# Layer 1 of a four-layer graph network: first operands in five pieces, a part's sums issued in front of the dense layers, and stepwise digits in the preparation

## The chip, the cores and the metric

The kernel runs on one core of one Trainium2 chip. The metric is the device time of one execution in microseconds (us), of which lower is better. Three timed executions of the kernel before took 5485.16, 5464.78 and 5445.3 us, so the median is 5464.78. The profile is of a further execution, with a time of its own that is given below.

A core has a tensor engine (PE, with its weight loads shown apart as PEld), a vector engine (DVE), a scalar engine (ACT), GpSimd (POOL) and a sync engine (SP), which here only issues transfers. Each works through its own queue of instructions in order and waits for the others by semaphores.

## The reference

Four graph layers run one after the other on node features x (3125 x 128, f32) and one list of 100000 edges, sorted by destination. Each is added to its input and normalised:

```python
edge_index = jnp.stack([src, dst])
x = layernorm(x + L0(x, z, edge_index, edge_type_500, Wc, P, y, residual_weight))
x = layernorm(x + L1(x, edge_index, W1, b1, W2, b2))
x = layernorm(x + L2(x, edge_index, edge_attr_3, Wq, Wk, Wv, We, Wo, bo, Wm, bm))
x = layernorm(x + L3(x, edge_index, edge_type_8, node_type_4, W_Q, W_K, W_V, W_edge, mu))
```

L0 is attention with 8 heads and an embedding for each of 500 relations: every edge has a logit from its destination's, its source's and its relation's vectors, a softmax runs over a node's incoming edges and the node itself, and the messages are summed. L2 is attention with 4 heads and a bias from three edge attributes, L3 attention with a matrix for each node type and edge type. L1, which the change is mostly about, is a mean over the edges the other way round and a small network:

```python
row, col = edge_index[0], edge_index[1]          # row = src, col = dst
summed = segment_sum(x[col], row)
deg = segment_sum(ones, row)
agg = summed / maximum(deg, 1)[:, None]
return relu(agg @ W1.T + b1) @ W2.T + b2
```

## The kernel before, in words

All is one function, `tile_gnn`, written for a framework that orders the instructions. The function's text gives each instruction a priority in the order in which it is written. A block under `tc.high_priority(offset=AHEAD)`, with AHEAD = 600, is treated as if it stood 600 places earlier, as far as its inputs allow. Tiles come from pools; a tile name with `bufs=2` has two buffers, and a third use waits until the first is released. These rules, and the semaphores that follow from them, set the order on each engine.

**Preparation** (to about 200 us). Edges are sorted into a table `edge_table` by destination; `h_tab` and `z_tab` are tables of node and relation vectors, transformed for layer 0. Nodes are ordered by in-degree into NT = 25 tiles of 128. Tile t has CAP[t] edge slots to a node, from 57 down to 21, in columns OFF[t] to OFF[t+1]; NS = 821 in all. GpSimd gathers the edges of each tile (the payload, `pay_sb`, L504), SP stores all of it to `pay_tab` (L505), and VectorE derives from each tile's payload (L507 to L516) the source `srcx`, a mask, the relation `rel` and the source in a second form, `srcs`. Then, over all 821 columns at once, come L517 to L523: two additions, and the splitting of `srcs` into its low seven bits plus one (`srclo`) and the rest (`srchi`). L525 to L533 turn `rel` into floats (`relf`), transpose it in seven blocks of up to 128 columns on TensorE, convert each on ScalarE and store it to `rel_tab` by SP; two buffers `r16` take turns.

**Counting.** Layer 1 needs a matrix of how many edges lead from each source to each destination. `counts` (L574 to L658) makes it for one tile of destinations by one-hots (L582, L619), a scan (L586), scalings on ScalarE (L623) and matmuls, and stores it to `c_tab`. It is a generator: its steps are issued one by one between the gathers of layer 0.

**behind** (L660 to L686) is a loop over edges that don't fit in a node's slots. The number of trips is read from memory by all engines (`values_load`), so all of them meet there, at L666 and L667. With the given inputs it is zero. For layer 0 it is called at L927, in front of the counting and the tiles.

**Layer 0** (L757 to L1038, to about 2060 us). For each of 25 tiles, GpSimd gathers the rows of sources from `h_tab`, one instruction to a slot (all gathers are recorded at L102); part of the relation vectors come by gathers too, part by one-hot matmuls from `rb`, which SP loads from `rel_tab`. After softmax and layernorm a tile's result goes to `x1_tab`, and its product with W1, split into three bf16 pieces, to `u_tab` (L1038).

**Layer 1** (L1042 to L1163, to about 2239 us). `u1` is all of `u_tab` (L1044, one transfer). A branch (L1057) leads to a general path for graphs for which the counts don't fit; it isn't taken here. Then come the weights: `w2` and its transpose, the bias rows `b1` and `b2`, and `wqkv2` for layer 2. The out-degree becomes `deg1` (L1123), is transposed (`dT`) and stored as one row, `degrow` (L1131); `xn` is the layer's input (L1133). The 3200 columns of sources are worked through in seven parts, CW = 512 columns each and 128 in the last. For each part the counts `cs` are loaded (L1137, two buffers), and 1 + 75 matmuls add up in `y_ps` (two buffers): `b1` times `degrow` (L1140), then 25 tiles x 3 pieces (L1143). VectorE and ScalarE make `hT` of it (L1145, L1146). Each 128 columns then go through the dense layers: a matmul with `w2T` (`o_ps`, L1150), the residual and a layernorm into `xq` (two buffers), a transpose, a matmul with `wqkv2` (`p_ps`), and two stores to `kv_tab` and `xq_tab` (L1162, L1163).

**Layers 2 and 3** gather from these tables and are not touched. Layer 2 opens with gathers of `xqb` from `xq_tab`.

Of the kernel before, what the change touches and what calls it, by code (L numbers as in the profile page):

```python
# [8 lines left out]
F32 = mybir.dt.float32  # L9
F16 = mybir.dt.float16  # L10
BF16 = mybir.dt.bfloat16
I32 = mybir.dt.int32
AF = mybir.ActivationFunctionType
OP = mybir.AluOpType
# [4 lines left out]
P = 128  # L19
N = 3125  # L20
NT = 25
NP = NT * P
# [9 lines left out]
PADREL = 511  # L32
# [10 lines left out]
OFF = [sum(CAP[:t]) for t in range(NT + 1)]  # L43
NS = OFF[NT]
# [7 lines left out]
CW = 512  # L52
NCW = -(-NP // CW)
AHEAD = 600
# [33 lines left out]
def tile_gnn(ctx, tc, a, out):  # L88
    nc = tc.nc
    V, A, G, T = nc.vector, nc.scalar, nc.gpsimd, nc.tensor  # L90
# [22 lines left out]
    ident = const.tile([P, P], F32, name="ident")  # L113
# [378 lines left out]
    rel = slots.tile([P, NS], I32, name="rel")  # L492
    srcx = late.tile([P, NS], I32, name="srcx")
    srclo = slots.tile([P, NS], F32, name="srclo")
    srchi = slots.tile([P, NS], BF16, name="srchi")
    pay_tab = dram.tile([P, NS * PW], I32, name="pay_tab")
    rel_tab = dram.tile([-(-NS // P) * P, P], F16, name="rel_tab")
    with tc.tile_pool(name="srcp", bufs=1) as sp, tc.tile_pool(name="srcq", bufs=2, space=PSUM) as ps:

        pay_sb = sp.tile([P, NS, PW], I32, name="pay_sb")  # L500
        start_i = sp.tile([P, NT], I32, name="start_i")
        V.tensor_copy(start_i, od.start)
        for t in range(NT):
            gather(pay_sb[:, OFF[t]:OFF[t + 1], :].rearrange("p s w -> p (s w)"), edge_tab, start_i[:, t:t + 1])  # L504
        nc.sync.dma_start(pay_tab, pay_sb.rearrange("p s w -> p (s w)"))  # L505
        srcs = sp.tile([P, NS], I32, name="srcs")
        for t in range(NT):  # L507
            sl = slice(OFF[t], OFF[t + 1])
            V.tensor_copy(srcx[:, sl], pay_sb[:, sl, 0])
            live = sp.tile([P, max(CAP)], F32, name="live", bufs=2)  # L510
            V.tensor_scalar(live[:, :CAP[t]], slotid[:, :CAP[t]], od.deg[:, t:t + 1], None, op0=OP.is_lt)
            V.tensor_scalar(mask[:, sl], live[:, :CAP[t]], -NEG, NEG, op0=OP.mult, op1=OP.add)
            V.scalar_tensor_tensor(rel[:, sl], pay_sb[:, sl, 1], float(-PADREL), live[:, :CAP[t]],
                                   op0=OP.add, op1=OP.mult)
            V.scalar_tensor_tensor(srcs[:, sl], pay_sb[:, sl, 0], float(-NP), live[:, :CAP[t]],
                                   op0=OP.add, op1=OP.mult)  # L516
        V.tensor_scalar(rel, rel, float(PADREL), None, op0=OP.add)  # L517
        V.tensor_scalar(srcs, srcs, float(NP), None, op0=OP.add)
        digit = sp.tile([P, NS], I32, name="digit")
        V.tensor_scalar(digit, srcs, 127, None, op0=OP.bitwise_and)  # L520
        V.tensor_scalar(srclo, digit, 1.0, None, op0=OP.add)
        V.tensor_scalar(digit, srcs, 7, None, op0=OP.arith_shift_right)
        V.tensor_copy(srchi, digit)  # L523

        relf = sp.tile([P, NS], F32, name="relf")  # L525
        V.tensor_copy(relf, rel)
        for o in range(0, NS, P):
            n = min(P, NS - o)
            rps = ps.tile([P, P], F32, name="rps")
            T.transpose(rps[:n], relf[:, o:o + n], ident)  # L530
            r16 = sp.tile([P, P], F16, name="r16", bufs=2)
            A.activation(r16[:n], rps[:n], AF.Copy)
            nc.sync.dma_start(rel_tab[o:o + n], r16[:n])  # L533


    c_tab = dram.tile([NCW * P, NT * CW], BF16, name="c_tab")
# [235 lines left out]
    u_tab = dram.tile([P, NT * 3 * D], BF16, name="u_tab")  # L772
# [3 lines left out]
    with tc.tile_pool(name="l0", bufs=2) as wp, tc.tile_pool(name="l0s", bufs=1) as sp, \  # L776
# [147 lines left out]
            spread(ac, hs, lg[:, :W], W)  # L924
            nc.sync.dma_start(sums_at[t], az)

        behind(wp, behind0)  # L927

        up = count_up(cp, ps1)

# [6 lines left out]
        done = 0.0  # L937
        x1st = own(0)
        ahead = x1st, prologue(0, x1st)
        for t in range(NT):  # L940
            n = CAP[t]
# [7 lines left out]
            for run in runs(t):  # L949
                hss = []  # L950
                for s0, w, mult in run:
                    o = OFF[t] + s0
                    if s0 + w == n and t + 1 < NT:

                        ahead = x_next, prologue(t + 1, x_next)
# [85 lines left out]

    with ExitStack() as ctx1, tc.tile_pool(name="l1", bufs=2) as wp, tc.tile_pool(name="l1s", bufs=1) as sp:  # L1042
        u1 = sp.tile([P, NT, 3, D], BF16, name="u1")
        nc.sync.dma_start(u1, u_tab.rearrange("p (t k d) -> p t k d", t=NT, k=3))  # L1044

        more = sp.tile([P, 1], F32, name="more")
        V.tensor_reduce(more, crowd, AX.X, OP.max)
# [9 lines left out]
        with tc.If(general > 0):  # L1057

            with tc.tile_pool(name="l1g", bufs=1) as gp, tc.tile_pool(name="l1gp", bufs=1, space=PSUM) as ps:
# [13 lines left out]
                for t in range(NT):  # L1073
# [27 lines left out]
                    for c in range(NCW):  # L1101
                        w = min(CW, NP - c * CW)
# [5 lines left out]
                for c in range(NCW):  # L1108
                    w = min(CW, NP - c * CW)
# [21 lines left out]
        nc.sync.dma_start(degrow, dT)  # L1131
        xn = sp.tile([P, NT, D], F32, name="xn")
        nc.sync.dma_start(xn, x1_tab.rearrange("(t p) d -> p t d", p=P))  # L1133
        for c in range(NCW):
            w = min(CW, NP - c * CW)
            cs = wp.tile([P, NT, CW], BF16, name="cs")
            nc.sync.dma_start(cs[:, :, :w], c_tab[c * P:(c + 1) * P].rearrange("p (t w) -> p t w", w=CW)[:, :, :w])  # L1137
            y_ps = ps1.tile([P, CW], F32, name="y_ps", bufs=2)

            T.matmul(y_ps[:, :w], b1, degrow[:, c * CW:c * CW + w], start=True, stop=False)  # L1140
            for t in range(NT):
                for k in range(3):
                    T.matmul(y_ps[:, :w], u1[:, t, k, :], cs[:, t, :w], start=False, stop=(t == NT - 1 and k == 2))  # L1143
            hT = wp.tile([P, CW], F32, name="hT")
            V.tensor_add(hT[:, :w], y_ps[:, :w], sums[:, c * CW:c * CW + w])  # L1145
            A.activation(hT[:, :w], hT[:, :w], AF.Relu)  # L1146
# [28 lines left out]
    with tc.tile_pool(name="l2", bufs=2) as wp, tc.tile_pool(name="l2s", bufs=1) as sp, \  # L1175
# [105 lines left out]
        for t in range(NT):  # L1281
            qp = query(ps1, qb[:, t, :])
            for s0, s1, run in segments(t):
                lg = wp.tile([P, max(CAP), H2], F32, name="lg")
                parts = []
                for c0, w in run:
                    o = OFF[t] + c0
# [126 lines left out]
```

## Time and profile before

| what | value |
|---|---|
| timed executions, median | 5464.78 us (5445.3 to 5485.16) |
| profiled execution, its own time | 4502.25 us |
| its span | 4500.4 us |
| instructions | 40304 |
| busy: PE, PEld | 2014.7 us (45%), 1312.7 us (29%) |
| busy: DVE, ACT, POOL | 3035.2 us (67%), 973.0 us (22%), 2845.9 us (63%) |
| mean granted clock of TensorE | 0.699 of full speed |
| transfers | 498.40 MB, mean 111 GB/s |

The stages, as starts of the work of each show them in the timeline (us from the span's start):

| stage | from | to |
|---|---|---|
| preparation | 0 | 200.4 |
| layer 0, with the counting beside it | 200.4 | 2060 |
| layer 1 | 2060 | 2239 |
| layer 2 | 2239 | 3404 |
| layer 3 | 3404 | 4500 |

How to read the profile's lines that follow. In a timeline a line has the start in us, the duration (from the first to the last of a bundle when it ends in "x2" or more), the engine, the line of the source, the operation, what it writes and reads, and, in brackets, how long the engine had waited and for whom. An engine's name with a q, as SPq or ACTq, is its own queue or sequencer: issues of transfers, register reads and branches. In a table of windows each engine has its busy time in the stretch and its number of instructions. Releasers are inferred from semaphores. The profiled execution is over 900 us shorter than the timed ones, and the profile does not say where that lies.

### The profile page before, as it was taken

The numbers are of one execution on the slowest core, as the hardware profiler recorded it, in microseconds if no ns is written. First come the engines' busy times: TensorE is split into PE (matmuls) and PEld (weight loads), VectorE is DVE, ScalarE is ACT, GpSimd is POOL, SyncE is SP. The second block draws the span as 40 slices with busy tenths as digits, with TensorE's granted clock in tenths as the row PEclk, the third lists the DMA queues.
The fourth block names the chain that finished last, engine by engine and source line by source line (L and its number), as shares of the span: only waits on it lengthen the run. The fifth ranks groups of instructions, "written<-read, shape, count | busy, mean of one in ns | idle before, by whom it ended". The sixth has DMA issues, their size and how long they took to land. (4 is left out here: it accounts for less than half of the span.)

```text
span 4500.4 us, 40304 instructions
## 1 busy us (share of the span) xinstructions
PE 2014.7 (45%) x12091; PEld 1312.7 (29%) x12091; DVE 3035.2 (67%) x7206; ACT 973.0 (22%) x2553; POOL 2845.9 (63%) x2897
## 2 busy tenths in 40 slices
PE   6458678877797787896802223233331000000000
PEld 5245455655565465563300011111110000000000
DVE  8649679887788697883336776777762556566566
ACT  0124334433344343331101111111110000000000
POOL 0376546666677365560077777777755777777775
PEclk9678789888898798897955556566665555555555
DMA  2444333434344233354433443344432333333332
GB/s 70 134 115 118 98 88 104 122 108 114 102 132 123 70 113 99 90 129 169 147 97 113 121 129 121 121 129 129 129 105 90 104 104 104 104 103 103 104 102 75
DMA packets 213054, 498.40 MB, mean 111 GB/s; under 512 B 62329, under 2 KB 109100, under 8 KB 208185
## 3 DMA queue, kind: packets, MB, share of 16 engines
q0 software_dynamic: 136448, 397.65, 30.9%
q1 hardware_dynamic: 76344, 97.76, 6.8%
q8 instruction: 102, 1.67, 0.2%
q14 instruction: 160, 1.31, 0.1%
HBM read 424.65 MB, written 70.63 MB: 110 GB/s over the span
## 5 line engine op out<-in xcount | busy, mean ns | idle before, releaser
L102 POOL DMA_INDIRECT hs<-h_tab,srcx x821 | 898.5, 1094 | 552.3 <-issue 346.4
L102 POOL DMA_INDIRECT kv<-kv_tab,pay_sb x821 | 781.3, 952 | 257.8 <-issue 249.3
L102 POOL DMA_INDIRECT kv<-ktv_tab,pay_sb x821 | 777.4, 947 | 263.9 <-issue 258.4
L1351 DVE TENSOR_TENSOR qk<-kv,qp 128x1024 f32<-128x1024 f32 (+4 forms) x114 | 126.8, 1112 | 465.8 <-DMA kv<-ktv_tab,pay_sb 391.8
L728 DVE TENSOR_REDUCE u<-msg 128x128 f32<-128x1024 f32 (+4 forms) x228 | 382.7, 1678 | 0.0
L879 PE MATMUL zps<-oh,zq 128*128 128x512 bf16 x1232 | 365.2, 411 | 34.6 <-DVE oh L870 34.1
L1193 DVE TENSOR_TENSOR qk<-kv,qp 128x1024 f32<-128x1024 f32 (+4 forms) x114 | 126.8, 1113 | 341.4 <-DMA kv<-kv_tab,pay_sb 324.1
L891 PE MATMUL t_ps<-zw,zT 128*128 128x136 f32 x1232 | 210.6, 299 | 113.5 <-DVE hs L892 94.6
L102 POOL DMA_INDIRECT zs<-z_tab,rel x205 | 216.1, 1054 | 64.3 <-issue 56.5
L623 ACT ACTIVATE c_oha<-c_oha,srclo 128x50 bf16<-128x50 bf16 (+2 forms) x821 | 202.3, 327 | 221.0 <-DVE c_oha L619 216.8
L724 DVE TENSOR_TENSOR msg<-kv,ex 128x1024 f32<-128x1024 f32 (+4 forms) x228 | 248.2, 1101 | 0.0
L830 PE MATMUL lg<-yw,low 128*128 128x8 f32 x1642 | 219.1, 260 | 26.2 <-ACT low L828 16.8
L830 PEld LDWEIGHTS lg<-yw,low 128*128 128x128 f32 x1642 | 210.5, 199 | 67.7 <-ACT low L828 51.1
L739 PE MATMUL tp<-ident,an 128*128 128x128 f32 x25 | 11.5, 459 | 486.2 <-DVE an L1239 486.2
L891 PEld LDWEIGHTS t_ps<-zw,zT 128*128 128x128 f32 x1232 | 183.2, 202 | 146.0 <-DVE hs L892 106.3
L883 PE MATMUL pre<-zT,zw 128*128 128x512 f32 x308 | 188.6, 697 | 35.2 <-ACT zT L881 34.6
L885 PEld LDWEIGHTS pre<-ident,hs 128*128 128x128 f32 x1232 | 175.8, 208 | 66.6 <-issue 65.5
L828 ACT ACTIVATE low<-pre 128x512 f32<-128x512 f32 (+2 forms) x215 | 123.0, 573 | 299.5 <-PE pre L885 233.0
L885 PE MATMUL pre<-ident,hs 128*128 128x128 f32 x1232 | 181.1, 292 | 0.0
L821 PE MATMUL pre<-identb,hq 128*128 128x512 bf16 (+3 forms) x645 | 180.3, 372 | 1.3 <-ACT hq L813 0.7
L1263 PE MATMUL xk_ps<-of,xqb 128*128 128x512 f32 x50 | 50.9, 1121 | 278.9 <-DVE xqb L757 270.6
L879 PEld LDWEIGHTS <-zq 128*128 128x128 bf16 x1232 | 128.8, 112 | 121.2 <-issue 61.3
(395 smaller groups left out, 5172.4 us busy)
## 6 DMA issues: line engine op xcount, KB each, us to landing
rb<-rel_tab SPq DMA_DIRECT2D x77, 256.0 KB, 3.3
c_tab<-c_sb SPq DMA_DIRECT2D x25, 768.0 KB, 3.7
cs<-c_tab SPq DMA_DIRECT2D x6, 3200.0 KB, 11.2
hs<-h_tab,srcx POOLq DMA_INDIRECT x821
kv<-kv_tab,pay_sb POOLq DMA_INDIRECT x821
kv<-ktv_tab,pay_sb POOLq DMA_INDIRECT x821
h_tab<-h SPq DMA_DIRECT2D x25, 132.0 KB, 2.3
zs<-z_tab,rel POOLq DMA_INDIRECT x205
```

The lines of the kernel that those rows point to most:

```text
L102: return G.indirect_dma_start(out=dst, out_offset=None, in_=table, in_offset=indirect(idx), **kw)
L623: A.activation(oha[:, s, 0, :], oha[:, s, 1, :], AF.Copy, scale=srclo[:, o:o + 1])
L724: V.tensor_tensor(msg[:, :n, :].rearrange("p s (h d) -> p s h d", h=heads), val.rearrange("p s (h d) -> p s h d", h=heads), ex.unsqueeze(3 ...
L728: V.tensor_reduce(u, msg[:, :n, :].rearrange("p s d -> p d s"), AX.X, OP.add)
L821: T.matmul(pre[:, :k], hq[:, i, :], identb.unsqueeze(1).to_broadcast([P, k, P]), start=(i == 0), stop=False)
L830: T.matmul(lg_ps[:, s, :], low[:, s, :], yw8, start=True, stop=True)
L879: T.matmul(zps, zq[:, i, 2 * R * k2:2 * R * (k2 + 1)], ohs[i][:, cols], start=(i + k2 == 0), stop=(i == NK - 1 and k2 == 1))
L883: T.matmul(pre[:, :k], zw[:, :D], zT[:, cols], start=False, stop=False)
L885: T.matmul(pre[:, s, :], hs[:, s0 + s, :D], ident, start=False, stop=(s == k - 1))
L891: T.matmul(t_ps[:, s, :], zT[:, (s0 + s) * P:(s0 + s + 1) * P], zw[:, D:], start=True, stop=True)
L1193: V.tensor_mul(qk[:, :n], kv[:, :n, :D], qp.unsqueeze(1).to_broadcast([P, n, D]))
L1351: V.tensor_mul(qk[:, :n], kv[:, :n, :D], qp.unsqueeze(1).to_broadcast([P, n, D]))
```

## The change

Three places are edited.

**Preparation.** The work of L517 to L533 becomes a function `digits_of(o, e)`, which does it for columns o to e: relations with their transposes and stores first, then the digits. It is called inside the loop over tiles, whenever another 256 columns are complete, and for the rest after the last tile: 0 to 256, 256 to 512, 512 to 768, 768 to 821.

**The call of `behind`** for layer 0 is put under `tc.high_priority(offset=AHEAD)`.

**Layer 1.** `u1` and the counts of the first part (`cs0`) are loaded in five pieces of five tiles each, in turns, ahead of the branch to the general path. The loading of `cs` and the sums of a part become a function `part(c)`, which returns `y_ps`; the sums of part c + 1 are issued ahead of the dense layers of part c.

```diff
--- before.py
+++ after.py
@@ -504,6 +504,27 @@
             gather(pay_sb[:, OFF[t]:OFF[t + 1], :].rearrange("p s w -> p (s w)"), edge_tab, start_i[:, t:t + 1])
         nc.sync.dma_start(pay_tab, pay_sb.rearrange("p s w -> p (s w)"))
         srcs = sp.tile([P, NS], I32, name="srcs")
+        digit = sp.tile([P, NS], I32, name="digit")
+        relf = sp.tile([P, NS], F32, name="relf")
+
+        def digits_of(o, e):
+
+            V.tensor_scalar(rel[:, o:e], rel[:, o:e], float(PADREL), None, op0=OP.add)
+            V.tensor_copy(relf[:, o:e], rel[:, o:e])
+            for q in range(o, e, P):
+                n = min(P, e - q)
+                rps = ps.tile([P, P], F32, name="rps")
+                T.transpose(rps[:n], relf[:, q:q + n], ident)
+                r16 = sp.tile([P, P], F16, name="r16", bufs=2)
+                A.activation(r16[:n], rps[:n], AF.Copy)
+                nc.sync.dma_start(rel_tab[q:q + n], r16[:n])
+            V.tensor_scalar(srcs[:, o:e], srcs[:, o:e], float(NP), None, op0=OP.add)
+            V.tensor_scalar(digit[:, o:e], srcs[:, o:e], 127, None, op0=OP.bitwise_and)
+            V.tensor_scalar(srclo[:, o:e], digit[:, o:e], 1.0, None, op0=OP.add)
+            V.tensor_scalar(digit[:, o:e], srcs[:, o:e], 7, None, op0=OP.arith_shift_right)
+            V.tensor_copy(srchi[:, o:e], digit[:, o:e])
+
+        done = 0
         for t in range(NT):
             sl = slice(OFF[t], OFF[t + 1])
             V.tensor_copy(srcx[:, sl], pay_sb[:, sl, 0])
@@ -514,23 +535,11 @@
                                    op0=OP.add, op1=OP.mult)
             V.scalar_tensor_tensor(srcs[:, sl], pay_sb[:, sl, 0], float(-NP), live[:, :CAP[t]],
                                    op0=OP.add, op1=OP.mult)
-        V.tensor_scalar(rel, rel, float(PADREL), None, op0=OP.add)
-        V.tensor_scalar(srcs, srcs, float(NP), None, op0=OP.add)
-        digit = sp.tile([P, NS], I32, name="digit")
-        V.tensor_scalar(digit, srcs, 127, None, op0=OP.bitwise_and)
-        V.tensor_scalar(srclo, digit, 1.0, None, op0=OP.add)
-        V.tensor_scalar(digit, srcs, 7, None, op0=OP.arith_shift_right)
-        V.tensor_copy(srchi, digit)
-
-        relf = sp.tile([P, NS], F32, name="relf")
-        V.tensor_copy(relf, rel)
-        for o in range(0, NS, P):
-            n = min(P, NS - o)
-            rps = ps.tile([P, P], F32, name="rps")
-            T.transpose(rps[:n], relf[:, o:o + n], ident)
-            r16 = sp.tile([P, P], F16, name="r16", bufs=2)
-            A.activation(r16[:n], rps[:n], AF.Copy)
-            nc.sync.dma_start(rel_tab[o:o + n], r16[:n])
+
+            whole = OFF[t + 1] if t == NT - 1 else OFF[t + 1] // (2 * P) * 2 * P
+            if whole > done:
+                digits_of(done, whole)
+                done = whole
 
 
     c_tab = dram.tile([NCW * P, NT * CW], BF16, name="c_tab")
@@ -924,7 +933,8 @@
             spread(ac, hs, lg[:, :W], W)
             nc.sync.dma_start(sums_at[t], az)
 
-        behind(wp, behind0)
+        with tc.high_priority(offset=AHEAD):
+            behind(wp, behind0)
 
         up = count_up(cp, ps1)
 
@@ -1041,7 +1051,11 @@
 
     with ExitStack() as ctx1, tc.tile_pool(name="l1", bufs=2) as wp, tc.tile_pool(name="l1s", bufs=1) as sp:
         u1 = sp.tile([P, NT, 3, D], BF16, name="u1")
-        nc.sync.dma_start(u1, u_tab.rearrange("p (t k d) -> p t k d", t=NT, k=3))
+        cs0 = wp.tile([P, NT, CW], BF16, name="cs")
+        for t0 in range(0, NT, 5):
+
+            nc.sync.dma_start(u1[:, t0:t0 + 5], u_tab.rearrange("p (t k d) -> p t k d", t=NT, k=3)[:, t0:t0 + 5])
+            nc.sync.dma_start(cs0[:, t0:t0 + 5], c_tab[:P].rearrange("p (t w) -> p t w", w=CW)[:, t0:t0 + 5])
 
         more = sp.tile([P, 1], F32, name="more")
         V.tensor_reduce(more, crowd, AX.X, OP.max)
@@ -1131,16 +1145,28 @@
         nc.sync.dma_start(degrow, dT)
         xn = sp.tile([P, NT, D], F32, name="xn")
         nc.sync.dma_start(xn, x1_tab.rearrange("(t p) d -> p t d", p=P))
-        for c in range(NCW):
+
+        def part(c):
+
             w = min(CW, NP - c * CW)
-            cs = wp.tile([P, NT, CW], BF16, name="cs")
-            nc.sync.dma_start(cs[:, :, :w], c_tab[c * P:(c + 1) * P].rearrange("p (t w) -> p t w", w=CW)[:, :, :w])
+            cs = cs0 if c == 0 else wp.tile([P, NT, CW], BF16, name="cs")
+            if c:
+                nc.sync.dma_start(cs[:, :, :w], c_tab[c * P:(c + 1) * P].rearrange("p (t w) -> p t w", w=CW)[:, :, :w])
             y_ps = ps1.tile([P, CW], F32, name="y_ps", bufs=2)
 
             T.matmul(y_ps[:, :w], b1, degrow[:, c * CW:c * CW + w], start=True, stop=False)
             for t in range(NT):
                 for k in range(3):
                     T.matmul(y_ps[:, :w], u1[:, t, k, :], cs[:, t, :w], start=False, stop=(t == NT - 1 and k == 2))
+            return y_ps
+
+        ahead = part(0)
+        for c in range(NCW):
+            w = min(CW, NP - c * CW)
+            y_ps = ahead
+            if c + 1 < NCW:
+
+                ahead = part(c + 1)
             hT = wp.tile([P, CW], F32, name="hT")
             V.tensor_add(hT[:, :w], y_ps[:, :w], sums[:, c * CW:c * CW + w])
             A.activation(hT[:, :w], hT[:, :w], AF.Relu)
```

## The prediction

> **What bounds the kernel now.** I read the page first, then the busy time of the engines by stage, the timeline at the two places that the change touches, and the waits. The page's chain of work that ended last goes back only to about 3500 us, into layer 3; it reaches neither edited place, so their worth has to be read from the timeline there.
>
> Busy time by stage (columns: the stretch in us, its length, then for each engine busy us and instructions, then TensorE's granted clock, DMA share, GB/s):
>
> ```profile
> 145.00:178.00 33.00, 1.36 (x4) 0.41 (x4) 20.20 (x149) 0.28 (x1) 23.80 (x25) 0.50 0.51 151
> 178.00:200.40 22.40, 2.66 (x9) 1.35 (x9) 20.80 (x36) 3.11 (x12) 0.00 (x0) 0.50 0.36 136
> ...
> 2060.00:2239.00 179.00, 147.17 (x666) 67.96 (x666) 49.39 (x216) 24.00 (x83) 2.77 (x1) 0.89 0.49 177
> 2239.00:3404.00 1165.00, 305.26 (x578) 137.17 (x578) 758.18 (x1693) 169.97 (x373) 829.71 (x871) 0.58 0.39 120
> ```
>
> From 178 to 200.4 us VectorE works alone (20.80 of 22.40) while GpSimd, which must gather all of layer 0's rows, does nothing. Layer 1, 2060 to 2239, is TensorE's (147.17 of 179). Layers 2 and 3 are left as they were. The timeline of the first place:
>
> ```profile
> 178.25 0.18 DVE L509 COPY srcx<-pay_sb 128x21 int32<-128x21 int32 x1 [1.20 <-DMA pay_sb<-edge_table,start_i]
> ...
> 182.55 0.92 DVE L582 TENSOR_TENSOR c_oh<-srchi,each_j 128x1425 bf16<-128x1425 bf16 x1
> ...
> 194.60 2.35 DVE L586 TENSOR_TENSOR_SCAN c_inc<-c_oh 128x1050 f32<-128x1050 bf16 x1
> ...
> 198.83 1.35 ACT L623 ACTIVATE c_oha<-c_oha,srclo 128x75 bf16<-128x75 bf16 x5 [7.96 <-DVE c_oha L619]
> ...
> 200.46 0.35 POOL L798 MEMSET x<- 128x128 f32 x2 [24.32 <-ACTq L667]
> ```
>
> The engines meet at the loop of `behind` (L667); ScalarE comes last, with counting work, at 200.2, and GpSimd starts layer 0 after 24.32 us of waiting. The second place:
>
> ```profile
> 2060.54 0.32 SPq L1044 DMA_DIRECT2D u<-u_tab  x1
> ...
> 2073.16 3.42 SPq L1131 DMA_DIRECT2D degrow<-dT  x1
> 2076.62 30.89 SPq L1137 DMA_DIRECT2D cs<-c_tab  x3
> 2081.20 5.14 DVE L1151 TENSOR_TENSOR xn<-xn,b 128x128 f32<-128x128 f32 x25 [8.07 <-DMA xn<-x_tab]
> 2081.56 0.50 PEld L1140 LDWEIGHTS y_ps<-degrow,b 1*128 1x128 f32 x2 [9.04 <-DMA degrow<-dT]
> ...
> 2088.95 19.73 PE L1143 MATMUL y_ps<-cs,u 128*128 128x512 bf16 x82 [3.61 <-DMA cs<-c_tab]
> ```
>
> A part's first matmul is L1140, with `degrow`; the first sum (L1143) waits last for `cs`, issued only at 2076.62. Two transfers thus open layer 1, 7 us apart. At its end:
>
> ```profile
> 2218.76 0.69 DVE L1145 TENSOR_TENSOR hT<-y_ps,sums 128x512 f32<-128x512 f32 x1 [10.28 <-PE y_ps L1143]
> ...
> 2234.99 0.32 SPq L1163 DMA_DIRECT2D xq_tab<-xq  x1
> ...
> 2239.01 0.99 POOL L102 DMA_INDIRECT xqb<-xq_tab,node_d  x1 [175.35 <-issue]
> ```
>
> **What the Trainium skill says.** "DMA: Bandwidth & Descriptors", section "Queues, rings and completion order": an engine's descriptors are taken in ring order on each DMA engine, so a small load queued behind a big one comes after it. The trace agrees: the 64 KB bias load issued behind `u1` (2400 KB) took 8.7 us to land, a 128 KB store later 1.7. "Runtime: NRT & Kernel Launch", section "Instruction fetch mechanics": a taken branch to a page not held stalls for its fetch by DMA. The trace agrees: TensorE's jump over the general path (L1057), with `u1` under way, took 6.47 us, those at L329 and L1326 3.50 and 4.63. "TensorE: Matmul & The Clock Gate", Part 1: idle TensorE falls to half clock. The trace agrees: 0.50 in 2060 to 2089, 1.00 from 2107 to 2219.
>
> **The change part by part.** Its instruction order on each engine can be read without running it.
>
> Steps of preparation (L517 to L533). Before, seven full-width operations of 0.58 to 0.59 us, begun 0.50 to 0.61 apart, stand between the last payload (178.25) and the counts' first one-hot (182.55): 4.3 us. After, three of four steps (256 columns) run in VectorE's gaps between payloads. A 256-wide operation I put at 0.28 us (0.18 at 21 columns, 0.58 at 821, a straight line). The third step is held up: its order puts it behind the copy of payload 23, which lands at 176.57; 0.6 us of small operations and seven wide ones, of which two follow the last payload, give a one-hot at about 179.6. Gain 2.9 us.
>
> `behind` in front. VectorE no longer does before the meeting: the 1050-wide scan 2.35, three copies and a subtraction 0.57, three one-hots 0.69 + 0.78 + 0.68: 5.1 us; nor ScalarE its five scalings (1.35). VectorE leaves at 199.65 - 2.9 - 5.1 + 0.9 (the last step's 53-column operations, now between others) = 192.6. The queue of SP: `pay_tab` (2463 KB, 8.0 us) is still issued at 178.5; four of the seven `rel_tab` stores now go ahead of it, the fifth and sixth land behind it at about 187, the seventh waits for a buffer until then and lands at 189.5; `rb`, 3.3 us, lands at 192.9. So the meeting is at 193 to 193.5, not 200.2, and GpSimd starts **6.7 us** earlier. The 5.1 us go behind the meeting, where VectorE stood idle 4.43 us (for `rb`) and 3.88 (for the first rows) and was busy only 36.84 us of 200 to 300, against GpSimd's 76.74. That hides them; without that cover they cost 5.1. From the second tile on the order of layer 0 is the same on every engine, so I carry the shift through: -6.7.
>
> Five pieces. `u1` and part 0's `cs`, 5.73 MB in ten DMAs, go ahead of everything. `u1` flowed at about 0.42 MB/us from 2062.5; so they end at 2076.2. SP's ten issues and two waits for landed pieces bring it to its own jump at 2067 (2063.4 before), past it at 2070 to 2073. Then come `w2`, the biases and `wqkv` behind the pieces: `w2` lands at 2077.5 (about 2071.5 before). TensorE transposes it, then `deg1`; `dT` is ready at 2079.3, `degrow` is issued at 2079.6 and, behind the `xn` load (5.7 us of transfer after 2078.3), lands at 2085.5 instead of 2081.5. L1140 takes 1.9 us at half clock, and the sums begin at 2087.4: **-1.5** against 2088.95. What was late is no longer `cs` but `degrow`. Bounds: -8 (`degrow` does not suffer: 2081), +3 (SP's jump waits for all pieces). Later `cs` parts are issued with a buffer's release and take 11.2 us, under a part's 16: no stall.
>
> Sums in front. The work is the same; only the filling moves. Before, a part ends every 22.4 us with four dense tiles between its sums; without them it takes 75 x 0.213 + 1.1 = 17.1. One part now runs bare: part 5 ends 5.3 us earlier, 6.8 with the start, at 2211.9. But nine dense tiles then remain with only part 6's 4.8 us of short matmuls to cover them, not five. Before, pairs of tiles were stored at 2224.93/2226.32, 2230.04/2231.49 and the single one at 2234.99: 5.0 us a pair (two `xq` buffers), 16.3 us from part 5's end. After: the first pair 4.8 us after the end, the single one 4 pairs later: 4.8 + 20 = 24.8. Layer 1 thus changes by -6.8 + 24.8 - 16.3 = **+1.7**; with TensorE idling towards half clock I take 2.5.
>
> Sum: -6.7 + 2.5 = **-4.2 us**. The profiled execution took 4502.25 us (span 4500.4 and 1.85 around it): 4498. The three timed runs have a median of 5464.78, 962 more, with 40 us between them; the profile does not show where those 962 lie, so I carry the microseconds over: **5461**.
>
> **The rivals.**
> Larger gain: `degrow` slips in early and the dense tiles overlap as pairs of pairs. Then -8 at the start, 4 off the tail: about -16, 5449. Against it: ring order, which delayed `w2` before.
> Slower: layer 1's tail. A tile at half clock costs more (the last `p_ps` took 1.65 us instead of 0.91, a transpose and an output matmul twice theirs: +1.4 a tile). Pairs then take up to 7.8 us, the tail 36, layer 1 +13, the whole **+6**: 5471. It decides from a pair of 6.1 us on. For it: while interleaved, pairs took about 8 us. Against it: at the end before, 5.0.
> Clock: part sums at half clock throughout would cost 450 x 0.213 = 96 us, 5560. Against it: layer 1 ran at 1.00 from 2107 to 2219.
> Change without effect in preparation: the meeting waits for SP's stores behind `pay_tab` as long as before; then only +2.5. This lies inside the forecast's range.
>
> **How the numbers follow.** Forecast (-10 to +3) 0.55; larger gain 0.15; slower tail 0.20; lower clock 0.04; a gain over 1% by a shift in layer 0 that I don't see 0.06. A measurement of this kernel can tell about 1% (55 us) from no change. Hence faster 0.06, within 1% 0.90, slower 0.04. With both tail cases (-16, +6) and some 15 to 20 us of scatter in a median of such runs, the range is 5430 to 5488.
>
> **What would show it.** Right: GpSimd's first memset of layer 0 near 193.5 after a wait of 17 us; the last `rel_tab` store near 187; in layer 1 the first sum waiting for `degrow`, not `cs`; nine dense tiles after the last full part. Wrong: first sum before 2080 (after the shift) or after 2092; layer 0 not 6 to 7 us earlier at its end; a half clock in the part sums.

## The result: no difference that the measurement can tell

The changed kernel takes 5472.66 us (median of 20 runs, 5445.61 to 5494.59), the kernel before 5458.85 (20 runs, 5424.51 to 5485.16). The ratio is 1.0016 with a 95% interval of 0.9999 to 1.0033, so the change costs between nothing and 18 us. In a second comparison (g11 below) it is 1.0005 (0.9986 to 1.0024). The forecast of 5461 and its range hold the time; the first interval leaves no room for the forecast gain of 4.2 us (0.9992), the second does not exclude it.

One thing must be known to read the traces: the same kernel runs at one of two levels, a "short" one (first trace: 4500.4 us) and a "long" one (second trace: 5463.9 us), whatever the change. Layer 1, 178.5 us in the first trace, is 177.8 in the second; layer 0 is 1860 and 2497. So every ratio and every absolute time below is compared within one level.

Busy time by stage of the kernel before in its second trace, e1 below (columns as in the prediction):

```profile
178.00:203.70 25.70, 2.52 (x9) 1.19 (x9) 23.25 (x57) 3.11 (x12) 0.03 (x1) 0.50 0.31 119
2700.00:2878.50 178.50, 147.12 (x666) 67.95 (x666) 49.41 (x216) 24.04 (x83) 2.77 (x1) 0.89 0.49 178
2878.50:4228.00 1349.50, 313.09 (x578) 139.02 (x578) 785.09 (x1698) 170.32 (x374) 830.38 (x871) 0.57 0.33 104
```

The same of the changed kernel:

```profile
178.00:198.10 20.10, 1.30 (x5) 0.59 (x5) 17.99 (x70) 0.76 (x3) 0.01 (x1) 0.50 0.38 147
2692.00:2876.00 184.00, 145.90 (x666) 68.75 (x666) 49.05 (x215) 24.05 (x83) 2.76 (x1) 0.89 0.49 172
2876.00:4221.00 1345.00, 308.22 (x578) 137.19 (x578) 785.73 (x1698) 170.75 (x374) 828.22 (x871) 0.57 0.34 104
```

VectorE does 5.3 us less between 178 us and layer 0's start (17.99 against 23.25), and this stretch is 5.6 us shorter. Layer 1 is some 6 us longer (184.0 against 177.8, first issue to first gather) with the same work in it. In these two stages the change thus gives about as much as it takes. The timeline of the changed kernel at the first place:

```profile
183.85 0.16 DVE L530 COPY srcx<-pay_sb 128x21 int32<-128x21 int32 x1
184.85 0.90 DVE L591 TENSOR_TENSOR c_oh<-srchi,each_j 128x1425 bf16<-128x1425 bf16 x1
...
198.09 0.34 POOL L807 MEMSET x<- 128x128 f32 x2 [21.06 <-DVEq L676]
...
201.92 2.35 DVE L595 TENSOR_TENSOR_SCAN c_inc<-c_oh 128x1050 f32<-128x1050 bf16 x1 [4.54 <-DMA az<-sums_tab]
```

The second scan (2.35 us) has moved behind GpSimd's first memset, which waited 21.06 us instead of 27.0 in the kernel before at this level. The start of layer 1, SP's issues and TensorE:

```profile
2692.27 0.32 SPq L1057 DMA_DIRECT2D u<-u_tab  x1
...
2697.61 0.58 SPq L1058 DMA_DIRECT2D cs<-c_tab  x1
2706.18 0.34 SPq L343 DMA_DIRECT2D w<-in_L_gnn_W  x1
...
2713.55 3.37 SPq L1145 DMA_DIRECT2D degrow<-dT  x1
2721.84 2.07 PE L1157 MATMUL y_ps<-degrow,b 1*128 1x512 f32 x2 [8.63 <-DMA degrow<-dT]
2723.84 18.98 PE L1160 MATMUL y_ps<-cs,u 128*128 128x512 bf16 x75
```

`degrow` is what TensorE waits for, 8.63 us; the sums then follow without a wait for the counts. And the end of layer 1:

```profile
2849.78 0.69 DVE L1171 TENSOR_TENSOR hT<-y_ps,sums 128x512 f32<-128x512 f32 x1 [10.29 <-PE y_ps L1160]
...
2872.25 0.32 SPq L1189 DMA_DIRECT2D xq_tab<-xq  x1
...
2876.28 0.99 POOL L102 DMA_INDIRECT xqb<-xq_tab,node_d  x1 [180.89 <-issue]
```

22.5 us lie between the last full part's result and the last store of `xq`, where the kernel before had 16.2.

### The profile page after: what moved, and what is told of

The parts are those of the page before. It is cut to its first block, busy times and chain, and to the rows that moved or that the text cites. A ratio compares the mean times of both kernels' runs of the same rounds, so it can differ in the third digit from the quotient of the medians.

```text
span 5449.7 us, 40327 instructions
## 1 busy us (share of the span) xinstructions
PE 2158.4 (40%) x12091; PEld 1396.4 (26%) x12091; DVE 3093.7 (57%) x7227; ACT 975.8 (18%) x2553; POOL 2810.8 (52%) x2897
## 5 line engine op out<-in xcount | busy, mean ns | idle before, releaser
L102 POOL DMA_INDIRECT hs<-h_tab,srcx x821 | 842.9, 1027 | 824.6 <-issue 482.5
L102 POOL DMA_INDIRECT kv<-ktv_tab,pay_sb x821 | 801.8, 977 | 322.6 <-issue 262.1
L888 PE MATMUL zps<-oh,zq 128*128 128x512 bf16 x1232 | 392.6, 436 | 68.0 <-DVE oh L879 49.4
L839 PE MATMUL lg<-yw,low 128*128 128x8 f32 x1642 | 237.5, 271 | 94.3 <-issue 48.4
L901 DVE TENSOR_TENSOR hs<-hs,t_ps 128x408 f32<-128x408 f32 (+1 forms) x231 | 121.6, 526 | 266.1 <-PE t_ps L900 98.0
L839 PEld LDWEIGHTS lg<-yw,low 128*128 128x128 f32 x1642 | 230.4, 215 | 139.4 <-ACT low L837 68.2
L656 PE MATMUL c_ps<-c_ohs,c_ohd 128*128 128x128 bf16 x1300 | 138.9, 260 | 257.6 <-ACT c_sb L658 116.2
L579 DVE TENSOR_TENSOR c_ohs<-c_ends,c_up 128x1024 bf16<-128x1024 bf16 (+3 forms) x196 | 115.6, 591 | 203.8 <-remote 153.7
L830 PE MATMUL pre<-identb,hq 128*128 128x512 bf16 (+3 forms) x645 | 201.8, 409 | 10.0 <-ACT low L837 9.4
L656 PEld LDWEIGHTS <-c_ohd 128*128 128x128 bf16 x1300 | 114.4, 118 | 317.9 <-issue 221.6
```

Of the source, the lines that this page charges most:

```text
L102: return G.indirect_dma_start(out=dst, out_offset=None, in_=table, in_offset=indirect(idx), **kw)
L656: T.matmul(cps[:, j * P:(j + 1) * P], ohd[:, b // 2, :, b % 2], ohs[:, b // 2, :, b % 2], start=(i == 0), stop=(i == nb - 1))
L830: T.matmul(pre[:, :k], hq[:, i, :], identb.unsqueeze(1).to_broadcast([P, k, P]), start=(i == 0), stop=False)
L839: T.matmul(lg_ps[:, s, :], low[:, s, :], yw8, start=True, stop=True)
L888: T.matmul(zps, zq[:, i, 2 * R * k2:2 * R * (k2 + 1)], ohs[i][:, cols], start=(i + k2 == 0), stop=(i == NK - 1 and k2 == 1))
```

## The experiments

Four numbers are read from each trace: GpSimd's first memset of layer 0 ("memset"), and for layer 1, counted from the first issue of `u`, the first sum ("start"), from there to the sixth part's `hT` ("middle"), and on to layer 2's first gather ("tail"). In f7 and g9 SP issues the small loads ahead of `u`; these 2.5 us are not counted in "layer 1".

| kernel | level | memset | start | middle | tail | layer 1 | ratio to the kernel before (95%) |
|---|---|---|---|---|---|---|---|
| before, first trace | short | 200.46 | 28.4 | 129.8 | 20.3 | 178.5 | |
| before again (e1) | long | 203.67 | 27.8 | 129.8 | 20.3 | 177.8 | 0.9993 (0.9978 to 1.0007) |
| changed | long | 198.09 | 31.6 | 125.9 | 26.5 | 184.0 | 1.0016 (0.9999 to 1.0033) |
| changed again (g11) | long | 199.28 | 30.5 | 124.7 | 27.4 | 182.6 | 1.0005 (0.9986 to 1.0024) |
| layer 1's part alone (e2) | long | 203.58 | 30.8 | 124.8 | 27.4 | 183.0 | 1.0009 (0.9993 to 1.0026) |
| preparation's part alone (e3) | long | 196.78 | 27.6 | 129.3 | 19.6 | 176.5 | 0.9998 (0.9981 to 1.0015) |
| `behind` alone (e4) | long | 203.66 | 27.1 | 129.7 | 19.4 | 176.2 | 0.9992 (0.9977 to 1.0006) |
| pieces alone (f5) | short | 200.58 | 32.0 | 130.7 | 19.2 | 181.9 | 1.0009 (1.0002 to 1.0016) |
| sums in front alone (f6) | short | 200.93 | 27.8 | 124.3 | 26.5 | 178.6 | 0.9997 (0.9989 to 1.0006) |
| changed, small loads ahead (f7) | short | 194.71 | 27.2 | 126.3 | 28.9 | 182.3 | 0.9997 (0.9987 to 1.0007) |
| steps alone (f8) | short | 195.64 | 26.8 | 129.4 | 19.4 | 175.6 | 0.9991 (0.9984 to 0.9998) |
| f7, bias last (g9) | long | 199.04 | 8.1 | 134.4 | 26.8 | 169.3 | 1.0001 (0.9987 to 1.0015) |
| g10, below | long | 198.69 | 8.4 | 144.7 | 20.0 | 173.2 | 0.9990 (0.9976 to 1.0004) |
| g12, below | long | 198.16 | 8.5 | 139.5 | 19.3 | 167.3 | 0.9966 (0.9950 to 0.9983) |

### e1: the kernel before once more

> The kernel before, unchanged. Two profiled executions were 950 us apart (span 4500 before, 5450 after), the timed ones only 14. Theory: the 950 us belong to the execution that was profiled, not to the change, so a further profile of the kernel before spans about 5450, with layer 0 near 2490 us instead of 1860 and layer 1 (first piece of u issued to GpSimd's first gather of layer 2) still near 178. Rival: the change itself makes layers 0, 2 and 3 longer; then this profile spans about 4500 again. Timed ratio 1.000.

The span was 5463.9 us, layer 0 (memset to `u`'s issue) 2497, layer 1 177.8. The theory holds: the 950 us aren't the change's. The ratio of 0.9993 is that of a kernel to itself, and shows how far noise alone can take it. Two traces of the changed kernel at this level have 2494 and 2495 us in layer 0.

### e2, e3, e4: the change in halves

e2 has only the edits of layer 1, e3 only those ahead of it, e4 only this one:

```diff
-        behind(wp, behind0)
+        with tc.high_priority(offset=AHEAD):
+            behind(wp, behind0)
```

> Only the layer 1 part of the change (five pieces, sums in front), preparation as before. Theory: layer 1 takes 184 us instead of 178.5 (the changed kernel's profile has 184.0): first sum 31 us after the first issue instead of 28.4, about 22 us from the end of part 5 to the last store instead of 16. Timed +5 us, ratio 1.001. Rival, the whole loss of 14 us comes from here: ratio 1.0025, with more than 190 us in layer 1.

Layer 1 took 183.0 us, of which the start 30.8 and the tail 27.4; ratio 1.0009, as the theory has it. More than 190 us isn't there.

> Only the preparation part (digits and relations in steps, the call of behind in front), layer 1 as before. Theory: GpSimd's first memset of layer 0 comes 6 to 7 us earlier than in the kernel before in an execution of the same kind, and layer 0 ends as much earlier; timed -6 us, ratio 0.999. Rival: the order of the counting steps that it moves makes layer 0 longer by more than it starts earlier; then ratio 1.001 to 1.002 (+5 to +10 us).

The memset came 6.9 us earlier than in e1. The ratio, 0.9998 (0.9981 to 1.0015), doesn't separate the two. In this trace layer 0 took 2509.9 us and ended 5.9 us later than in e1, in e4's it took 2480.7, in e1's and e2's 2497.1: single traces differ in layer 0 by more than this half of the change is worth. The rival stays open at the long level: layer 0 took 2494 to 2510 us in the six traces with this edit, 2481 to 2497 in the three without.

> Only the call of behind is put in front; digits and relations at full width, layer 1 as before. Theory: VectorE's 5.1 us of later counting work leave the stretch ahead of the meeting, ScalarE's five scalings too, but the seven stores of relations still stand behind the payload's store, so GpSimd's first memset comes 3 to 5 us earlier; ratio 0.999 to 1.000. Rival: the meeting is held by SP's stores anyway, the first memset comes at the same time, ratio 1.000.

Nothing moved, neither the memset (203.66 against 203.67) nor the work ahead of it. VectorE in e4:

```profile
197.80 2.35 DVE L586 TENSOR_TENSOR_SCAN c_inc<-c_oh 128x1050 f32<-128x1050 bf16 x1
...
201.91 0.68 DVE L570 TENSOR_TENSOR c_ohb<-c_digb,c_up 128x1024 bf16<-128x1024 bf16 x1
202.51 0.18 DVE L663 TENSOR_TENSOR cur<-start_d,caps 128x25 f32<-128x25 f32 x1
```

The scan, the copies and the one-hots still stand ahead of the loop's first operation (L663). The theory is wrong here, and the rival gives the right time for another reason: it isn't SP's stores that hold the meeting (GpSimd's wait of 26.95 us ends with ScalarE, as before), it is that the edit alone changes nothing in VectorE's order.

### f8: the steps alone

> Only the digits and relations in steps; the call of behind where it was, layer 1 as before. Theory: the steps alone already let nearly all of the later counting slip behind the meeting (in the order of VectorE only the second scan, 2.35 us, stays ahead of it), so GpSimd's first memset comes at 198.5 to 200 against 203.7 for the kernel before and 196.8 for steps and behind together. Rival, the split of the prediction: steps give 2.9 us and no more, 200.8.

```profile
192.59 0.17 DVE L672 TENSOR_TENSOR cur<-start_d,caps 128x25 f32<-128x25 f32 x1
192.68 0.18 DVE L674 TENSOR_TENSOR left<-deg_d,caps 128x25 f32<-128x25 f32 x1
192.78 0.18 DVE L615 TENSOR_SCALAR c_posi<-c_pos 128x57 int32<-128x57 f32 x1
192.88 2.34 DVE L595 TENSOR_TENSOR_SCAN c_inc<-c_oh 128x1050 f32<-128x1050 bf16 x1
```

This is the timeline of f8, at the short level: the loop's first operations (L672, L674) have slipped in front of the scan, the one-hots and copies are behind the meeting, and only the scan is left. The expected figures were of the long level; at the short one the memset is at 195.64 against 200.58 and 200.93 in f5 and f6, whose preparation is that of before. The steps alone thus give 5.1 us, with `behind` (f7) it is 6.0: once the steps are there, `behind` adds 0.9. GpSimd's wait then ends with SP (after 16.87 us), in f8 with VectorE (18.43). The ratio 0.9991 (0.9984 to 0.9998) is a gain of 4 us, in an interval that only just excludes none; it speaks for a gain that reaches the end of the kernel.

### f5 and f6: the two edits of layer 1, each alone

f5 takes over the ten loads of pieces, f6 the function `part(c)` with the sums issued ahead.

> Only the five pieces of u and of part 0's counts, ahead of the branch; sums and dense layers in the old order, preparation as before. Theory: all that the changed kernel loses at the start of layer 1 comes from here, because w2 and the biases, which stood ahead of SP's branch, stand behind it now, and degrow behind them: first sum 31 us after the first issue instead of 27.5, the tail from part 5's end to layer 2's first gather as before, 19.5 to 20.3; layer 1 180 to 181.5 instead of 176 to 178. Rival: pieces alone start the sums earlier (under 27), and it is the sums in front that delay the start.

```profile
2060.26 0.32 SPq L1047 DMA_DIRECT2D u<-u_tab  x1
...
2074.01 0.34 SPq L343 DMA_DIRECT2D w<-in_L_gnn_W  x1
...
2081.42 3.39 SPq L1135 DMA_DIRECT2D degrow<-dT  x1
2089.84 2.07 PE L1145 MATMUL y_ps<-degrow,b 1*128 1x512 f32 x2 [9.22 <-DMA degrow<-dT]
```

Start 32.0, middle and tail as before, layer 1 181.9. `w2` is issued 13.8 us after the first piece, `degrow` 21.2; in the kernel before it was 1.7 and 12.6. The pieces lose 4 to 5 us in layer 1, and the time shows it (1.0009, from 1.0002 to 1.0016).

> Only the sums of part c+1 issued ahead of the dense layers of part c; loads in the old place, preparation as before. Theory: start as before, 27 to 28; from the first sum to part 5's end 125 instead of 129.7; tail 26.5 to 27.5 instead of 20: layer 1 179 to 180.5. Rival: the second part's counts are not there in time when nothing stands between parts 0 and 1, and the middle stays near 130.

Start 27.8, middle 124.3, tail 26.5, layer 1 178.6. The middle gains 5 us, the tail gives 7 back. Both theories hold, and the two effects on layer 1 simply add up to that of the changed kernel. The ratio, 0.9997 (0.9989 to 1.0006), can't show the 2 us that remain.

### f7: the small loads ahead of the pieces

```diff
+        w2 = load(sp, a["L1_gnn_W2"], "w2")        # and b1, b2, wqkv2
         u1 = sp.tile([P, NT, 3, D], BF16, name="u1")
...
-        w2T = transposed(sp, ps1, load(sp, a["L1_gnn_W2"], "w2"), "w2T")
+        w2T = transposed(sp, ps1, w2, "w2T")
```

> The changed kernel with the loads of w2, b1, b2 and wqkv2 put ahead of the ten pieces. Theory: degrow's chain (w2, its transpose, that of the degree, degrow's store) is what the sums wait for, and SP's place decides it: degrow is then issued right behind SP's branch, some 15 us after the first piece, and the first sum comes at 18 to 24 instead of 31.6; layer 1 172 to 177 instead of 184. Rival: degrow lands behind pieces and xn whatever stands ahead (ring order); then the first sum stays at 28 or later.

The start became 27.2, which is neither the theory's 18 to 24 nor quite the rival's 28. The lines show which half of the theory failed:

```profile
2071.43 0.75 SPq L1064 DMA_DIRECT2D u<-u_tab  x1
...
2076.30 0.41 PE L1142 MATMUL dT_ps<-ident,deg 128*25 128x128 f32 x1 [0.37 <-ACT w2T L750]
...
2079.36 0.71 SPq L1065 DMA_DIRECT2D cs<-c_tab  x1
2086.74 0.82 SPq L1148 DMA_DIRECT2D xn<-x_tab  x1
2090.48 1.95 SPq L1146 DMA_DIRECT2D degrow<-dT  x1
...
2096.60 0.49 PEld L1158 LDWEIGHTS y_ps<-degrow,b 1*128 1x128 f32 x2 [20.18 <-DMA degrow<-dT]
```

The degree is transposed 4.9 us after the first piece's issue, so the chain by way of `w2` is gone. But SP issues pieces until 8.6, its jump takes 5.1 us, and it comes to `xn` only at 15.3. From there to the issue of `degrow` pass another 3.7 us, which no wait in the trace accounts for, and 6.1 to TensorE. So 14 us lie between the degree and the issue of its row, all of them SP's, with the pieces ahead of it. Whether another engine's queue would have brought `degrow` earlier wasn't tried.

### g9: the bias product last

Since `degrow` can't be early, the sums are made not to need it:

```diff
-            T.matmul(y_ps[:, :w], b1, degrow[:, c * CW:c * CW + w], start=True, stop=False)
             for t in range(NT):
                 for k in range(3):
-                    T.matmul(y_ps[:, :w], u1[:, t, k, :], cs[:, t, :w], start=False, stop=(t == NT - 1 and k == 2))
+                    T.matmul(y_ps[:, :w], u1[:, t, k, :], cs[:, t, :w], start=(t == 0 and k == 0), stop=False)
+            T.matmul(y_ps[:, :w], b1, degrow[:, c * CW:c * CW + w], start=False, stop=True)
```

> The kernel of the run with the small loads ahead, and the bias product (b1 times degrow) moved from the front of each part's sums to their end. Theory: degrow was issued behind SP's branch and behind a wait for the last pieces, and nothing else held the sums (w2 and the degree were transposed 5.6 us after the first piece's issue): the first sum now comes 6 to 9 us after it instead of 27.2, and the sums run at the rate of the pieces; part 0 ends at 24 to 28 instead of 46.6, part 1 waits for its counts (issued 21 us in, 11 us of transfer) and ends near 50 instead of 63.9; layer 1 166 to 171 instead of 182.3. Rival: TensorE isn't past its own branch, or the pieces land late; then the first sum comes after 15, and layer 1 gains under 6.

TensorE in g9, with `u`'s first issue at 2697.43:

```profile
2701.61 0.45 PE L748 MATMUL tp<-ident,w 128*128 128x128 f32 x1 [9.97 <-DVE rdeg L1140]
2705.50 0.59 PE L1160 MATMUL y_ps<-cs,u 128*128 128x512 bf16 x1 [3.44 <-DMA cs<-c_tab]
...
2706.09 17.18 PE L1160 MATMUL y_ps<-cs,u 128*128 128x512 bf16 x74
2723.33 1.12 PE L1161 MATMUL y_ps<-degrow,b 1*128 1x512 f32 x2
```

The first sum comes 8.1 us after the first issue, all 75 follow without a stop, and `degrow` is there when it is wanted. Layer 1 is 169.3 us, 13 less than in f7, inside the theory's figures. The start gains 19 us; 6 of them are lost again further on, for the middle is 8 us longer than in f7 (134.4 against 126.3). VectorE and TensorE after part 0's sums:

```profile
2723.01 5.14 DVE L1178 TENSOR_TENSOR xn<-xn,b 128x128 f32<-128x128 f32 x25 [16.40 <-DMA xn<-x_tab]
2728.07 0.68 DVE L1172 TENSOR_TENSOR hT<-y_ps,sums 128x512 f32<-128x512 f32 x1
...
2729.47 0.80 PE L1177 MATMUL o_ps<-w2T,hT 128*128 128x128 f32 x2 [5.03 <-ACT hT L1173]
...
2731.30 18.43 PE L1160 MATMUL y_ps<-cs,u 128*128 128x512 bf16 x75
```

Part 0's sums are ready at 2724.45, but VectorE is then busy with additions to `xn`, whose load was late, and makes `hT` 3.6 us later; TensorE, which has a matmul with `hT` in front of part 1's sums, waits 5.03 us for it. Part 1's counts, issued at 2719.53, may not have been there much earlier: the trace doesn't separate the two. With the 2.5 us in which SP issues the small loads first, that is still 5 us less than before the change. The timed ratio, 1.0001 (0.9987 to 1.0015), shows nothing of these 5 and preparation's 5, which together would make 0.998; its interval just excludes that, and where they went stays open.

### g10 and g12: combinations

Both have three pieces (tiles 0 to 5, 5 to 13, 13 to 25), the small loads behind the first, the bias product last, and the sums in the old order. g10 also loads part 1's counts ahead of the branch and gives `xq` four buffers.

```diff
-        for t0 in range(0, NT, 5):
+        for t0, t1 in ((0, 5), (5, 13), (13, NT)):
+            if t0 == 0:                            # w2, b1, b2, wqkv2, behind the first pair
...
-        ahead = part(0)
-            y_ps = ahead
-                ahead = part(c + 1)
+            y_ps = part(c)
```

```diff
+        cs1 = wp.tile([P, NT, CW], BF16, name="cs")    # g10 alone
+        nc.sync.dma_start(cs1, c_tab[P:2 * P].rearrange("p (t w) -> p t w", w=CW))
-                xq = wp.tile([P, 2 * D], F32, name="xq")
+                xq = wp.tile([P, 2 * D], F32, name="xq", bufs=4)
```

> Preparation as in the changed kernel; layer 1 with three pieces, the small loads behind the first, part 1's counts loaded ahead of the branch too, the bias product last, the sums in the old order (a part's own sums, then its dense layers), and four buffers of xq instead of two. Theory: first sum 6 to 10 us after the first issue, part 1's end near 47 to 52 (67 in the kernel before), middle as before otherwise, tail of five dense tiles 13 to 18 instead of 19.4 to 20.3: layer 1 150 to 160 instead of 176 to 178; with 5 to 6 us of preparation the time is 22 to 32 us under the kernel before, ratio 0.993 to 0.996. Rival: what is gained at the start is given back at the parts' counts, which come one transfer at a time; then layer 1 stays above 168 and the ratio above 0.997.

Layer 1 took 173.2 us, which is the rival's. Part 0's sums were done at 29 us, but then:

```profile
2728.90 7.93 PE L1162 MATMUL y_ps<-cs,u 128*128 128x512 bf16 x36 [1.63 <-DMA cs<-c_tab]
2742.94 2.07 PE L1163 MATMUL y_ps<-degrow,b 1*128 1x512 f32 x2 [6.11 <-DMA degrow<-dT]
```

With part 1's counts (3200 KB) ahead of it, `degrow` (one row) held part 0's result 6.11 us; SP's issue of it alone lasted 10.84 us. In g12, without that early load, the issue took 3.67 us and TensorE did not wait. The last stores show the other edit:

```profile
2866.92 0.32 SPq L1188 DMA_DIRECT2D xq_tab<-xq  x1
...
2868.30 0.32 SPq L1188 DMA_DIRECT2D xq_tab<-xq  x1
...
2869.75 0.32 SPq L1188 DMA_DIRECT2D xq_tab<-xq  x1
...
2871.20 0.32 SPq L1188 DMA_DIRECT2D xq_tab<-xq  x1
...
2877.72 0.32 SPq L1188 DMA_DIRECT2D xq_tab<-xq  x1
```

With four buffers, four tiles leave 1.4 us apart instead of in pairs (g12, with two buffers, has the pairs: 2852.39 and 2853.78, 2857.39 and 2858.84), but the fifth waits for part 6, whose sums now come later; the tail stays at 20.

> Preparation as in the changed kernel; layer 1 with three pieces, the small loads behind the first, the bias product last, and the sums in the old order, each part's ahead of its own dense layers; no early load of part 1's counts, two buffers of xq. Theory: degrow no longer stands behind an early load of counts, so part 0's result is there at 28 to 31 us after the first issue as with the bias last alone (30.6), part 1's near 53, then one part every 22.5, and a tail of 19.5 to 20.5 because only five dense tiles remain: layer 1 158 to 164, against 176 to 178 before and 182.6 to 184 in the changed kernel. With 5 us of preparation, 17 to 25 us under the kernel before, ratio 0.995 to 0.997. Rival: layer 0's own spread (15 us either way) hides it and the ratio stays within 0.998 to 1.001.

Layer 1 took 167.3 us, 3 more than expected: part 0's result is there at 31.7, but part 1's only at 57.6, not 53. Its sums begin as in g9 (34.6 us after the first issue, 33.9 there) and take 21.8 us instead of 18.4, because in the old order part 0's dense layers stand between them, which I had left out. The ratio is 0.9966 (0.9950 to 0.9983): 5441.13 us against 5460.44. This version is faster than the kernel before, and so than the changed one, which was not. Of the 19 us, 9 to 10 are layer 1 and 5 preparation by the traces; the rest is inside the interval. It combines three edits to layer 1 (fewer pieces with the small loads behind the first, the bias product last, the old order), so what each gives in it isn't measured.

### g11: the changed kernel once more

> The changed kernel itself, beside the others. Theory: its two halves cancel: preparation gives 5 to 6 us, layer 1 takes 5 to 7 (first sum at 31, tail 26 to 27), so ratio 0.9995 to 1.0010 against the kernel before. Rival: its timed difference of 14 us was real; ratio 1.002 or more.

Ratio 1.0005 (0.9986 to 1.0024), memset 4.4 us earlier than in e1, layer 1 182.6. Both ratios and the traces fit halves that about cancel; the rival's 1.002 lies inside the interval, so that a loss of some us more isn't excluded.

## Why the prediction was right and where it was wrong

The time lies in the range and within 1%, as forecast with 0.90. That says little for its mechanism: a range of 58 us also holds the unchanged time, and none of the three edits moved its stage by more than 7 us. The 962 us that were carried over unexplained turned out to be the distance of two levels at which the same kernel runs, so carrying them over was right by luck. The sum (-4.2 us) was off by some 5: by the traces preparation gives 4.4 to 6.9 and layer 1 costs 6.3 (means of 183.2 over three traces with the change, 176.9 over five without).

**Preparation: right in size, wrong in what does it.** Predicted -6.7; measured -5.6 and -4.4 in the changed kernel, -6.9 in e3, -6.0 at the short level (f7), the level of the profile that the prediction was made from. There the memset came at 194.71 after 16.9 us of waiting; predicted were 193.5 and 17. At the long level neither sign holds as an absolute time, since the payload itself is worked off 3 us later there (its last copy at 181.46 instead of 178.25 in the kernel before). The step "`behind` in front" (5.1 us of VectorE) is the one that failed: `behind` alone moves nothing (e4), the steps alone move all but the scan (f8). I read the order of the whole change and credited each shift to the nearest edit. Once the steps are there, it is worth 0.9 us (195.64 in f8, 194.71 in f7). The step "steps of preparation" was 2.9 us; the first one-hot came 2.1 us earlier at the short level (180.42 and 181.02 against 182.66 and 183.01). At the long one it came anywhere from 2.2 us earlier (183.53 in e3) to 0.3 later (186.02 in g11, against 185.75), for there the last payload's copy itself comes later with the steps, at 182.5 to 185.0 instead of 181.4 to 181.5. What the steps do besides, and the prediction gave to `behind`, is to let the later counting slip behind the meeting. (The seven wide operations begin 0.50 to 0.63 us apart, not to 0.61; the sum of 4.3 us is right.)

**Five pieces: the bottleneck was named rightly, the sign was wrong.** Predicted -1.5, bounds -8 and +3; measured +3.6 (mean start 31.2 in four traces with the pieces, 27.6 in six without). `degrow` did replace `cs` as the last wait. The terms that were mis-sized: SP past its jump, put at 9.5 to 12.5 us after the first issue, was at 13.9, the jump alone 6.5; `w2`, put at 17.0, was used at 19.7; and from `degrow`'s issue to TensorE's start I took 5.9 where 8.3 passed. "Runtime: NRT & Kernel Launch" in the Trainium skill, section "Instruction fetch mechanics", says that a taken branch can stall for its fetch; I had looked at TensorE's jumps (3.5 to 6.5 us) and took SP's at the low end, though the kernel before has one in the same place (6.2 us). There it counted for less, for `w2` was issued in front of it. The cost of the edit is thus ten issues that push a short load, and what hangs on it, behind a jump; f7 shows that with the load back in front, `degrow` is still late, by SP's own way to it.

**Sums in front: right.** Predicted -5.3 and +8.5; measured -4.8 in the middle and +7.3 at the end (means of four traces with the edit and six without), for the reason given: nine dense tiles remain where five did. The pairs took 4.2 to 4.6 us (stores at 2854.78, 2859.41, 2863.88, 2868.03, 2872.25), not 5.0. They go with the two buffers of `xq`: with four (g10) they are gone, with two in otherwise the same order (g12) they are there.

**The rivals.** The larger gain falls with the start. The slower tail is close in time (+6) but not in mechanism: it needs pairs of 6.1 us, and the pairs were shorter than in the kernel before. What it says of the clock is there in small: the tails of 26.5 us had a granted clock of 0.93 (changed) and 0.94 (f6), those of 27.4 had 0.84 (g11) and 0.83 (e2), that of 28.9 had 0.78 (f7). Half clock in the sums falls: 75 matmuls of the second part took 16.36 us, 0.22 each. A preparation without effect falls as well.

**The carrying through** of preparation's gain to the end can't be seen in single traces, where layer 0 spreads by 15 us either way: the prediction's sign, layer 0 ending 6 to 7 us earlier, can't be read there, and f8's own layer 0 ended at 2061.5, where those without the edit end at 2060.3 to 2069.8. f8's ratio supports it at the short level (4 of 5 us); at the long level, e3's 0.9998 and g9's 1.0001 leave it open.

## What to carry to other kernels

Splitting a load into pieces so that work can start early helps only if nothing else that the first instruction needs comes later: here a one-row operand at the front of the accumulation kept everything waiting, and moving its product to the end of the sum started the sums 19 us earlier and shortened layer 1 by 13. Count issues on the queue that must also take a branch, for what is pushed behind the jump pays for the jump. And when an edit is several, take the instruction order of each alone before crediting a shift to one of them.

## What of the hardware was not expected

- The same program ran at two levels: the kernel before had a median of 4513 us beside f5 to f8 and of some 5460 beside all the others. Layer 1 is equal in both, and the first 140 us within 1; layer 0 is 1860 and 2497 us, layers 2 and 3 together 2261 and 2585, and the busy time of VectorE (3035 and 3096) and GpSimd (2846 and 2815) hardly differs. The extra time is waiting, in the stages where GpSimd gathers rows. f5 to f8 ran on one chip and the other experiments on three others, so it may belong to the chip; what decides it wasn't tried.
- SP's jump over code that isn't run (its wait from the branch to its next instruction) took 5.6 to 6.3 us in layer 1 in the six traces with `u` as one transfer, 5.7 to 6.5 in the four with ten pieces and the small loads behind the jump, and 5.1 to 5.8 in f7, g9, g10 and g12, which load more ahead of it. The ranges overlap: how much is under way doesn't visibly set it.
- At the long level a single trace of layer 0 is good to some 15 us only; the ratio of two medians there is good to about 9.
